# Re-ordered loads and weight sums in the first steps of a recurrent network kernel

## The chip, the cores and the metric

The kernel runs on one core of a Trainium2 chip. The core has five engines with a queue of instructions each: TensorE (PE, matrix products), VectorE (DVE), ScalarE (ACT), GpSimd (POOL) and SyncE (SP, which here only issues transfers). Transfers (DMAs) are issued on the queues of SP, ACT and POOL. The metric is the time of one execution on the device in microseconds (us); lower is better.

## The reference

A gated recurrent network runs over 128 time steps for 64 sequences; input and state have 512 values. The result is the input plus the state after each step.

```python
def step(h, inp):
    x_t, prop = inp
    comb = jnp.concatenate([x_t, h], axis=-1)
    z = jax.nn.sigmoid(comb @ Wz + bz)
    r = jax.nn.sigmoid(comb @ Wr + br)
    comb2 = jnp.concatenate([x_t, r * h], axis=-1)
    h_cand = jnp.tanh(comb2 @ Wh + bh)
    h_new = (1.0 - z) * h + z * h_cand
    h_next = jnp.where(prop, jnp.tanh(h_new @ Wp + bp), h_new)
    return (h_next, h_new)
```

`prop` holds for every fourth step. Each of Wz, Wr and Wh is 1024 x 512: its upper half multiplies x (in the kernel `wx`, 1.05 MB for each gate), its lower half multiplies the state (`wh[0]` for R, `wh[1]` for Z, `wh[2]` for H, 1.05 MB each). All values are float32.

## The kernel before

**Layout.** The 64 sequences are two halves of 32. A tile has 128 partitions: four quarters (`part(q)`) of a matrix's rows or of the 512 values, with 32 partitions each. All matmuls write 32 partitions, so that several run side by side.

**Two kinds of PE work.** The recurrent part of step t needs the state of step t-1: gates R, Z and H (`gate`), then PE multiplies for the half while the other half is in ACT and DVE. The input part (x times `wx`) does not depend on the state. It is cut into *units*, kept in a list (`put`), and taken from it between the recurrent gates (`fill`); how many are taken where stands in `PLACES`, in `HEAD` for steps 0 to 4 and in `TAIL`. `both(n)` takes n units for both halves at once, ahead of step 0. For steps 0 to 3 the units are plain products (`plain`, four per gate and step). From step 4 on the input part of several steps is computed together by a scheme of fewer products over sums of steps and sums of weights (`batch`); the first of these batches run in steps 1 and 2.

**Weight sums.** The batches need sums and differences of parts of `wx`. `sum_outer_1` makes `d5` (shown as `d` in the profile), `sum_outer` makes `tw[3]`, `tw[2]`, `tw[4]` in this order, two operations of 128x768 each; `sum_inner` and `sum_inner_1` make three sums (`tt`) and a fourth (`din`, or in place) of one weight, 128x384 each. Sums of x (`sum_raw12` gives `s12r`, `sum_raw34` gives `s34r`) stand on POOL too. Sums of weights 1 and 2 are made by DVE, all others by POOL. POOL's sums of weights 3, 5 and the outer ones start inside step 0: in `join` at t = 0 a copy of one element into `held` makes POOL wait until DVE has finished weight 2. `held` is used for such waits in two more places.

**The start, in order.** SP and ACT issue x of steps 0 and 1 (eight loads), the x part of Wr in two halves, Wz, Wh, then `wh[R]`; POOL issues the biases, h, and, after a `held` that waits for Wz, x of steps 2 and 3. A load takes one of eight semaphores in turn and waits until the load that had it before has landed. PE first runs 52 products of zeros (`idle`), then R of steps 0 and 1, the products that spread the three bias rows over the partitions (`spread`; ACT copies them to `bias_x`), then Z and H of these steps. `add_bias` (DVE) adds the biases and leaves the input part in `cp`; `seed` (ACT) copies it to the gate's place in PSUM, ahead of the recurrent products. `join_x` (DVE) transposes x of a step. Then four units of step 2 and step 0 itself. The products of one step share three scratch banks; `r_`, the gate R, lies in the bank of `scratch_r`, which the H units of an even plain step use as well.

The order on each engine is the order of the program text: there is no scheduler. The loop at the end interleaves the two halves by the number of columns that each has multiplied.

Of the kernel before, what the change touches and what calls it, by code (L numbers as in the profile page):

```python
# [18 lines left out]
def kernel(  # L19
# [14 lines left out]
    nc = tc.nc  # L34
# [97 lines left out]

    nc.gpsimd.tensor_copy(held, wx[0:1, 0, Z, 0:1])
    load_x(xr[0], 2, 2, 2, (nc.gpsimd, nc.gpsimd))

    dummy = const.tile([1, 1], F32, name="dummy")
    nc.scalar.activation(dummy, ones[:, 0:1], AF.Sigmoid)

    def load_wh(i):
        load_w(wh[i], gates_in[i][D:], engs=both_queues)  # L140

    load_wh(R)

# [130 lines left out]
    def inner(i, ka, na):  # L274
        return OPERAND[i](ka)[:, :, :, ts(na, J // 4)]
# [14 lines left out]

    def sum_outer():
        for ka in range(S):
            nc.gpsimd.tensor_sub(tw[3][:, ka], outer(1, 1, ka), outer(0, 1, ka))
            nc.gpsimd.tensor_add(tw[2][:, ka], tw[3][:, ka], outer(0, 0, ka))
            nc.gpsimd.tensor_sub(tw[4][:, ka], outer(1, 0, ka), tw[2][:, ka])

# [3 lines left out]

    def sum_inner(i, eng):
        eng.tensor_sub(tt[:, i - 1, 1], inner(i, 1, 1), inner(i, 0, 1))
        eng.tensor_add(tt[:, i - 1, 0], tt[:, i - 1, 1], inner(i, 0, 0))
        eng.tensor_sub(tt[:, i - 1, 2], inner(i, 1, 0), tt[:, i - 1, 0])

    def sum_inner_1(i, eng):
        eng.tensor_sub(leftover(i), inner(i, 0, 1), inner(i, 0, 0))

# [296 lines left out]
    )  # L605
    HEAD = {0: (4, 8, 0), 1: (8, 6, 0), 2: (16, 12, 0), 3: (8, 6, 8), 4: (6, 8, 0)}
    TAIL = {
# [9 lines left out]

    def plain_two(i):
        put(sum(map(list, zip(*(plain(t, (i,)) for t in range(2)))), []))
        both(2 * K)  # L620
# [70 lines left out]
    def behind_r(t, duo, u):  # L691
        odd = FIRST + 2 * duo + 1
        if t == 2:
            pair_left(0, 1, 2)
        elif t == 3:
            pair_right(0, 1, 10)
            sum_inner(7, nc.gpsimd)
            sum_inner_1(7, nc.gpsimd)
        if t == 4:
            sum_inner(4, nc.gpsimd)  # L700
            sum_inner_1(4, nc.gpsimd)
        if u == 0 and duo >= 1 and odd - 2 < LAST:
            outer_u2(odd - 2)

    def join(t, duo, u, n):
        even, odd = FIRST + 2 * duo, FIRST + 2 * duo + 1
        if t == 0 and n == 0:
            sum_inner(2, nc.vector)
            sum_inner_1(2, nc.vector)
            nc.gpsimd.tensor_copy(held, leftover(2)[0:1, 0, 0, 0:1])  # L710
# [15 lines left out]
    def behind_step(t, duo, u, h_new):  # L726
# [5 lines left out]
        if t == 0:  # L732
            sum_outer()
        if t == 3:
# [69 lines left out]
    def half(h):  # L804

        for t in range(T):
# [27 lines left out]
            if h == 1:  # L834
# [6 lines left out]
                if t == 1:  # L841
                    sum_raw34(1)
                    sum_inner(6, nc.gpsimd)
                    sum_inner_1(6, nc.gpsimd)
                if last:
                    nc.gpsimd.tensor_sub(xr[g][:, j], xr[g][:, j], keep)
                if t == 0:
                    join_x(1, 0)
                    join_x(1, 1)
                    sum_raw12(1)  # L850
                    sum_inner(5, nc.gpsimd)
                    sum_inner_1(5, nc.gpsimd)
                if t == 2:
# [97 lines left out]
```

## Time and profile before

| | us |
|---|---|
| runs shown | 1275.31, 1275.43, 1278.18 (median 1275.43) |
| the profiled execution | 1274.24 |
| its span on the core | 1272.4 |
| granted clock of PE, mean over the span | 0.997 of full |

The profile's page and trace come from the one profiled execution. Lines of the profile have the line of the kernel, the engine, the operation, the tiles written and read (`out<-in`), the shape and a count. In the stretches, each engine's busy time is followed by the number of its instructions in brackets; then come the clock granted to PE as a share of full speed, the share of the DMA engines that was busy, and GB/s. In the timeline a row has its start, its length, the engine and, in square brackets, how long the engine had been idle and what ended that. In the list of waits stand the instruction that waited, what it waited for, the time in total, how often, and the longest. Rows of DMA issues have the queue (SPq, ACTq, POOLq), the number of issues, the size of each and the median time from issue to landing. A float32 product stands twice in the trace. The line of most products, transposes and activations is that of a helper (L214 products, L240 activations of a gate, L384 `seed`, L422 `add_bias`, L256 `join_x`, L302 to L307 inner sums, L293 to L295 and L299 outer sums, L315 to L318 sums of x, L94 and L100 loads), so tiles tell them apart.

### The profile page before, as it was taken

The numbers are of one execution on the slowest core, as the hardware profiler recorded it, in microseconds if no ns is written. First come the engines' busy times: TensorE is split into PE (matmuls) and PEld (weight loads), VectorE is DVE, ScalarE is ACT, GpSimd is POOL, SyncE is SP. The second block draws the span as 40 slices with busy tenths as digits, with TensorE's granted clock in tenths as the row PEclk, the third lists the DMA queues.
The fourth block names the chain that finished last, engine by engine and source line by source line (L and its number), as shares of the span: only waits on it lengthen the run. The fifth ranks groups of instructions, "written<-read, shape, count | busy, mean of one in ns | idle before, by whom it ended". The sixth has DMA issues, their size and how long they took to land.

```text
span 1272.4 us, 60714 instructions
## 1 busy us (share of the span) xinstructions
PE 1253.4 (99%) x25964; PEld 1163.3 (91%) x25964; DVE 769.1 (60%) x2155; ACT 835.1 (66%) x2685; POOL 899.1 (71%) x1043
## 2 busy tenths in 40 slices
PE   8899999999999999999999999999999999999997
PEld 4688899999999999999999999999999999999875
DVE  2455666566666666656666666666666666666554
ACT  1456666766667666666666666666666666667665
POOL 2989767777677787767787677876777777677530
PEclk9999999999999999999999999999999999999999
DMA  9302212101221111112111121111111111111010
GB/s 234 92 3 53 52 42 62 38 22 51 52 53 36 38 49 38 53 36 57 40 28 52 50 55 36 36 40 49 53 37 47 41 37 53 41 48 36 11 43 19
DMA packets 112980, 60.82 MB, mean 48 GB/s; under 512 B 12968, under 2 KB 108968, under 8 KB 112712
## 3 DMA queue, kind: packets, MB, share of 16 engines
q1 hardware_dynamic: 109988, 53.20, 16.0%
q8 instruction: 205, 3.36, 1.1%
q10 hardware_dynamic: 2212, 3.34, 1.0%
q0 software_dynamic: 512, 0.40, 0.1%
q14 instruction: 63, 0.52, 0.1%
HBM read 40.11 MB, written 16.78 MB: 45 GB/s over the span
## 4 chain that ended last, share of the span: by engine, by line
PE 90%; POOL 5%; DMA 3%; issue 1%; DVE 1%; ACT 1%; SPq 0%; POOLq 0%; DVEq 0%; ACTq 0%
PE rec L214 41%; PE rec_z L214 15%; PE scratch_r L214 12%; PE scratch_q L214 10%; PE scratch_a L214 4%; PE scratch_y L214 4%; PE scratch_x L214 3%; DMA wh<-in_L_cond_Wz_dram 1%; DMA wx<-in_L_cond_Wh_dram 1%; POOL cp L555 1%; POOL mb L560 1%; DMA xr<-in_x_dram 0%; DMA wh<-in_L_cond_Wh_dram 0%; ACT rec_z L240 0%; DMA wx<-in_L_cond_Wr_dram 0%
## 5 line engine op out<-in xcount | busy, mean ns | idle before, releaser
L214 PE MATMUL rec<-wh,rhT 128*32 128x256 f32 x4096 | 375.5, 379 | 0.1
L214 PE MATMUL rec<-wh,hT 128*32 128x256 f32 x3072 | 281.6, 379 | 1.3 <-DVE hT L243 1.3
L214 PE MATMUL rec_z<-wh,hT 128*32 128x256 f32 x3072 | 281.6, 379 | 0.1
L214 PEld LDWEIGHTS rec<-wh,rhT 128*32 128x32 f32 x4096 | 249.8, 110 | 19.1 <-ACT scratch_r L240 0.5
L240 ACT ACTIVATE scratch_r<-rec 64x128 f32<-64x128 f32 x512 | 128.0, 250 | 131.7 <-PE rec L214 66.3
L384 ACT COPY rec<-cp 64x256 f32<-64x256 f32 x512 | 189.8, 371 | 25.1 <-DVE cp L422 5.7
L214 PEld LDWEIGHTS rec_z<-wh,hT 128*32 128x32 f32 x3072 | 192.4, 110 | 9.0 <-ACT rec_z L384 0.6
L214 PEld LDWEIGHTS rec<-wh,hT 128*32 128x32 f32 x3072 | 186.4, 110 | 14.1 <-ACT c L240 3.2
L240 ACT ACTIVATE rec_z<-rec_z 64x128 f32<-64x128 f32 x512 | 128.0, 250 | 98.8 <-PE rec_z L214 86.7
L240 ACT ACTIVATE c<-rec 64x128 f32<-64x128 f32 x512 | 138.9, 271 | 60.2 <-PE rec L214 48.8
L779 POOL TENSOR_TENSOR xr<-xr,h 128x256 f32<-128x256 f32 x127 | 92.8, 731 | 92.9 <-DVE h L872 81.9
L555 POOL TENSOR_TENSOR mb<-mb,mb 128x768 f32<-128x768 f32 x58 | 106.2, 1831 | 67.1 <-DVE mb L521 67.1
L555 POOL TENSOR_TENSOR cp<-mb,mb 128x768 f32<-128x768 f32 x76 | 138.9, 1827 | 8.1 <-DVE mb L521 4.4
L555 POOL TENSOR_TENSOR cp<-mb 128x768 f32<-128x768 f32 x46 | 84.2, 1830 | 56.8 <-ACT rec_z L384 55.4
L837 DVE SCALAR_TENSOR_TENSOR keep<-rec_z,h 128x256 f32<-128x256 f32 x96 | 40.7, 424 | 133.8 <-ACT rec_z L240 129.6
L214 PE MATMUL scratch_r<-tw,s 128*32 128x192 f32 x928 | 120.8, 326 | 0.0
L494 ACT COPY cq<-scratch_q 128x384 f32<-128x384 f32 x212 | 102.0, 481 | 19.9 <-PE scratch_q L214 18.4
L511 DVE TENSOR_TENSOR cx<-scratch_r,cx 128x384 f32<-128x384 f32 x106 | 59.0, 557 | 87.2 <-PE scratch_r L214 76.0
L214 PE MATMUL scratch_q<-tt,s 128*32 128x192 f32 x928 | 103.6, 326 | 0.0
L517 DVE TENSOR_TENSOR mb<-scratch_q,cx 128x384 f32<-128x384 f32 x106 | 59.0, 557 | 57.8 <-ACT cq L494 57.6
L821 DVE TENSOR_TENSOR rh<-scratch_r,h 128x128 f32<-128x128 f32 x192 | 56.0, 292 | 60.1 <-ACT scratch_r L240 60.1
L214 PE MATMUL rec<-wh,hpT 128*32 128x256 f32 x992 | 91.4, 379 | 0.1
(185 smaller groups left out, 3822.9 us busy)
## 6 DMA issues: line engine op xcount, KB each, us to landing
out_dram<-xr SPq DMA_DIRECT2D x249, 64.0 KB, 1.8
xr<-in_x_dram SPq DMA_DIRECT2D x248, 64.0 KB, 2.0
xs<-in_x_dram SPq DMA_DIRECT2D x240, 64.0 KB, 2.1
wp<-in_L_cond_Wp_dram SPq DMA_DIRECT2D x4, 256.0 KB, 5.0
wx<-in_L_cond_Wr_dram SPq DMA_DIRECT2D x4, 128.0 KB, 3.2
wx<-in_L_cond_Wr_dram ACTq DMA_DIRECT2D x4, 128.0 KB, 3.3
wx<-in_L_cond_Wz_dram SPq DMA_DIRECT2D x2, 256.0 KB, 5.9
wx<-in_L_cond_Wz_dram ACTq DMA_DIRECT2D x2, 256.0 KB, 6.6
```

The lines of the kernel that those rows point to most:

```text
L214: nc.tensor.matmul(ps[part(2 * h + c)], lhsT=left, rhs=rhs(c), start=start, stop=True, skip_group_check=True,)
L240: nc.scalar.activation(dst[ts(d, 2 * V)], gate_ps(i, h)[ts(h, 2 * V), d, :], func)
L384: nc.scalar.copy(gate_ps(i, h)[rows].rearrange("p d (c n) -> p d c n", c=C), G[t][rows, :, :, i, :].rearrange("p c d n -> p d c n"),)
L494: nc.scalar.copy(c[:, :nm], ps[:, :nm])
L511: nc.vector.tensor_add(T2[what][:, :nm], r_ps[:, :nm], T2[what][:, :nm])
L517: nc.vector.tensor_add(blocks(1, 1), runs(q_ps[:, :nm]), runs(T2[what][:, :nm]))
L555: nc.gpsimd.tensor_add(dst, a, b)
L560: nc.gpsimd.tensor_add(m, m, v.unsqueeze(1).to_broadcast([P, 2, 3 * J]))
L779: nc.gpsimd.tensor_add(xr[g][:, j], xr[g][:, j], h_new)
L821: nc.vector.tensor_mul(rh[:, h, :], r_, h_old[:, h, :])
L837: nc.vector.scalar_tensor_tensor(out=keep, in0=z, scalar=1.0, in1=h_old, op0=ALU.subtract, op1=ALU.mult)
```

## The change

1. x of steps 0 to 3 is loaded step by step (`load_step`, four loads of 32 KB each): step 0 first on SP and ACT, then the first half of Wr, then step 1 and the biases on POOL's queue, then the second half of Wr, Wz and Wh. Steps 2 and 3 follow on SP and ACT behind Wh and ahead of `wh[R]`. h waits for the second half of Wr instead of x. The activation table is loaded ahead of Wz's issue.
2. PE's start: 48 products of zeros for 52; R of step 0 and of step 1, first half of the depth; the biases; R, second half. Z and H of steps 0 and 1 step by step.
3. The inner sums are four operations in one function and can be done for some gates only: DVE makes weights 1 and 2 for R and Z as soon as these are loaded, and for H later, all before step 0. DVE also makes `d5` there (`sum_outer_1`), and POOL's `held` waits for it; POOL then does weights 3 and 5 and `tw[3]` ahead of step 0's own work, and `tw[2]`, `tw[4]` behind step 0.
4. Step 2's units: R and Z, then step 3, then H of step 2. Six units for four ahead of step 0, six for eight at its end. The H input part of step 0 is copied (`seed`) inside step 0.

```diff
+    def load_step(t, engs=both_queues):
+        for q in (0, 2, 1, 3):
+            engs[q // 2].dma_start(
+                out=xr[0][part(q), t], in_=x[:, t, ts(q, J)].rearrange("(h b) u -> b h u", h=S)
+            )
+    software_queue = (nc.gpsimd, nc.gpsimd)
...
-    load_x(xr[0], 0, 2, engs=both_queues)
-    for k in range(0, K, 2):
-        load_w(wx[:, :, R, :], gates_in[R][:D], k, k + 2, both_queues)
+    load_step(0)
+    load_w(wx[:, :, R, :], gates_in[R][:D], 0, 2, both_queues)
+    load_step(1, software_queue)
+    for i, b in enumerate((br, bh, bz)):
+        nc.gpsimd.dma_start(out=bias_row[:, i, :], in_=b.rearrange("(o n) -> o n", o=1))
+    load_w(wx[:, :, R, :], gates_in[R][:D], 2, K, both_queues)
+    dummy = const.tile([1, 1], F32, name="dummy")
+    nc.scalar.activation(dummy, ones[:, 0:1], AF.Sigmoid)
     for i in (Z, H_):
         load_w(wx[:, :, i, :], gates_in[i][:D], engs=both_queues)
-    for i, b in enumerate((br, bh, bz)):
-        nc.gpsimd.dma_start(out=bias_row[:, i, :], in_=b.rearrange("(o n) -> o n", o=1))
...
-    nc.gpsimd.tensor_copy(held, xr[0][0:1, 1, 1, 0:1])
+    nc.gpsimd.tensor_copy(held, wx[0:1, 2, R, 0:1])
...
-    nc.gpsimd.tensor_copy(held, wx[0:1, 0, Z, 0:1])
-    load_x(xr[0], 2, 2, 2, (nc.gpsimd, nc.gpsimd))
...
-    load_wh(R)
...
-    HEAD = {0: (4, 8, 0), 1: (8, 6, 0), 2: (16, 12, 0), 3: (8, 6, 8), 4: (6, 8, 0)}
+    HEAD = {0: (4, 6, 0), 1: (8, 6, 0), 2: (16, 12, 0), 3: (8, 6, 8), 4: (6, 8, 0)}
...
-    idle(52)
+    first = {i: [plain(t, (i,)) for t in range(2)] for i in (R, Z, H_)}
+    idle(48)
     join_x(0, 0)
+    now(first[R][0][:2])
     join_x(0, 1)
-    plain_two(R)
+    now(first[R][1][:2])
     spread(scratch[3], slice(0, 2), (R, H_))
     spread(scratch[1], slice(2, 3), (Z,))
+    nc.gpsimd.tensor_sub(bias_d, bias_x[:, 1], bias0)
+    load_step(2)
+    now(first[R][0][2:] + first[R][1][2:])
     for t in range(2):
         add_bias(t, (R,))
     for h in range(S):
         seed(R, 0, h)
-    load_wh(Z)
-    nc.gpsimd.tensor_sub(bias_d, bias_x[:, 1], bias0)
+    load_step(3)
+    load_wh(R)
+    now(sum(first[Z], []))
+    for i in (1, 2):
+        sum_inner(i, nc.vector, slice(0, 2))
+    for t in range(2):
+        add_bias(t, (Z,))
+    seed(Z, 0, 0)
     hT = new_T("hT", "hT_init")
     for h in range(S):
         turn(hT[:, h, :], h_init[:, h, :])
-    plain_two(Z)
-    for t in range(2):
-        add_bias(t, (Z,))
-    seed(Z, 0, 0)
+    load_wh(Z)
     join_x(0, 2)
-    sum_inner(1, nc.vector)
-    sum_inner_1(1, nc.vector)
-    plain_two(H_)
+    for i in (1, 2):
+        sum_inner(i, nc.vector, slice(2, 3))
+    now(sum(first[H_], []))
     for t in range(2):
         add_bias(t, (H_,))
-    for h in range(S):
-        seed(H_, 0, h)
     join_x(0, 3)
+    sum_outer_1(nc.vector)
+    nc.gpsimd.tensor_copy(held, d5[0:1, 1, 0, 0, 0:1])
+    for i in (3, 5):
+        sum_inner(i, nc.gpsimd)
+    sum_outer(3)
     load_wh(H_)
     later_loads()
-    put(plain(2) + plain(3))
-    both(K)
+    put(plain(2, (R, Z)) + plain(3) + plain(2, (H_,)))
+    both(6)
...
-        if t == 0 and n == 0:
-            sum_inner(2, nc.vector)
-            sum_inner_1(2, nc.vector)
-            nc.gpsimd.tensor_copy(held, leftover(2)[0:1, 0, 0, 0:1])
-            sum_inner(3, nc.gpsimd)
-            sum_inner_1(3, nc.gpsimd)
-            sum_outer_1(nc.gpsimd)
-        elif t == 1:
+        if t == 1:
             join_x(1, 2 + n)
...
         if t == 0:
-            sum_outer()
+            sum_outer(2)
+            sum_outer(4)
...
-            if last:
+            if last or t == 0:
                 seed(H_, t, h)
```

`now(units)` puts units on the list and takes them at once. `sum_outer(n)` makes `tw[n]` alone. The calls of `sum_inner_1` go with the new `sum_inner`, and `sum_inner(5, nc.gpsimd)` inside step 0 is gone.

More of the change, by code (lines that the diff above doesn't have):

```diff
@@ L131 @@
         )
-    nc.gpsimd.tensor_copy(held, wx[0:1, 0, Z, 0:1])
-    load_x(xr[0], 2, 2, 2, (nc.gpsimd, nc.gpsimd))
-    dummy = const.tile([1, 1], F32, name="dummy")
-    nc.scalar.activation(dummy, ones[:, 0:1], AF.Sigmoid)
     def load_wh(i):
         load_w(wh[i], gates_in[i][D:], engs=both_queues)
-    load_wh(R)
     xs = {}
@@ L289, in factor, with sum_outer @@
         }[j]()
-    def sum_outer():
+    def sum_outer(n):
         for ka in range(S):
-            nc.gpsimd.tensor_sub(tw[3][:, ka], outer(1, 1, ka), outer(0, 1, ka))
-            nc.gpsimd.tensor_add(tw[2][:, ka], tw[3][:, ka], outer(0, 0, ka))
-            nc.gpsimd.tensor_sub(tw[4][:, ka], outer(1, 0, ka), tw[2][:, ka])
+            if n == 3:
+                nc.gpsimd.tensor_sub(tw[3][:, ka], outer(1, 1, ka), outer(0, 1, ka))
+            elif n == 2:
+                nc.gpsimd.tensor_add(tw[2][:, ka], tw[3][:, ka], outer(0, 0, ka))
+            else:
+                nc.gpsimd.tensor_sub(tw[4][:, ka], outer(1, 0, ka), tw[2][:, ka])
     def sum_outer_1(eng):
@@ L299, in sum_outer_1, with sum_inner, of @@
             eng.tensor_sub(d5[:, ka], outer(0, 1, ka), outer(0, 0, ka))
[L301 to L307, printed above, removed]
+    def sum_inner(i, eng, gates=slice(0, 3)):
+        def of(v):
+            return v[:, :, gates]
+        t = [of(tt[:, i - 1, n]) for n in range(3)]
+        v = {ab: of(inner(i, *ab)) for ab in ((0, 0), (0, 1), (1, 0), (1, 1))}
+        eng.tensor_sub(t[1], v[1, 1], v[0, 1])
+        eng.tensor_add(t[0], t[1], v[0, 0])
+        eng.tensor_sub(t[2], v[1, 0], t[0])
+        eng.tensor_sub(of(leftover(i)), v[0, 1], v[0, 0])
     sx = {}
@@ L616, in both, with now @@
                     pass
-    def plain_two(i):
-        put(sum(map(list, zip(*(plain(t, (i,)) for t in range(2)))), []))
-        both(2 * K)
-    idle(52)
+    def now(units):
+        put(units)
+        both(len(units))
+    first = {i: [plain(t, (i,)) for t in range(2)] for i in (R, Z, H_)}
+    idle(48)
     join_x(0, 0)
+    now(first[R][0][:2])
     join_x(0, 1)
-    plain_two(R)
+    now(first[R][1][:2])
     spread(scratch[3], slice(0, 2), (R, H_))
     spread(scratch[1], slice(2, 3), (Z,))
+    nc.gpsimd.tensor_sub(bias_d, bias_x[:, 1], bias0)
+    load_step(2)
+    now(first[R][0][2:] + first[R][1][2:])
     for t in range(2):
@@ L843, in half @@
                     sum_inner(6, nc.gpsimd)
-                    sum_inner_1(6, nc.gpsimd)
                 if last:
@@ L850, in half @@
                     sum_raw12(1)
-                    sum_inner(5, nc.gpsimd)
-                    sum_inner_1(5, nc.gpsimd)
                 if t == 2:
```

2 lines of the change are left out of this document (removed).

## The prediction

> **What bounds the kernel now.** I read the page first, then the waits of TensorE (PE) over the whole span, then the first 120 us by stretches, because the change only touches the start.
>
> ```profile
> span 1272.4 us, 60714 instructions
> PE 1253.4 (99%) x25964; PEld 1163.3 (91%) x25964; DVE 769.1 (60%) x2155; ACT 835.1 (66%) x2685; POOL 899.1 (71%) x1043
> PE scratch_y L214 <- POOL s34r L317: 4.0, 1, 4.0
> PE scratch_q L214 <- DMA wx<-in_L_cond_Wr_dram: 2.2, 2, 1.3
> PE scratch_x L214 <- POOL s4r L317: 1.1, 1, 1.1
> PE rec L214 <- ACT rec L384: 1.0, 1, 1.0
> PE scratch_q L214 <- DVE cp L422: 0.7, 1, 0.7
> PE scratch_r L214 <- DVE rh L821: 0.3, 1, 0.3
> ```
>
> PE is busy 99% of the span: only what PE loses by waiting or by running slowly can be won. The longest wait, 4.0 us, is for one sum that POOL makes (`s34r`). In the stretches below the columns are PE, weight loads, DVE, ACT and POOL busy, then the clock granted to PE, the share of the DMA engines, and GB/s.
>
> ```profile
> 0.00:7.00 7.00, 4.89 (x56) 1.87 (x60) 1.04 (x3) 0.00 (x0) 3.46 (x11) 1.00 0.60 169
> 7.00:14.15 7.15, 5.20 (x80) 2.56 (x80) 0.62 (x2) 2.49 (x6) 2.65 (x6) 1.00 1.03 264
> 14.15:19.00 4.85, 4.85 (x60) 3.24 (x64) 0.54 (x3) 0.66 (x2) 2.82 (x5) 0.65 1.06 253
> 19.00:26.10 7.10, 5.89 (x108) 3.46 (x99) 4.15 (x10) 0.75 (x3) 0.00 (x0) 1.00 1.06 292
> 35.00:56.00 21.00, 20.76 (x421) 15.54 (x412) 12.28 (x36) 12.01 (x40) 20.40 (x18) 1.00 0.37 95
> 56.00:61.00 5.00, 1.21 (x16) 0.80 (x20) 1.39 (x4) 0.00 (x0) 4.92 (x7) 0.85 0.26 72
> 61.00:66.00 5.00, 5.00 (x98) 3.65 (x94) 0.13 (x1) 0.96 (x2) 4.84 (x6) 0.81 0.13 33
> 66.00:110.00 44.00, 44.00 (x956) 39.16 (x952) 26.18 (x72) 27.26 (x87) 40.33 (x44) 1.00 0.14 35
> ```
>
> Three limits follow each other. Up to 26 us the loads decide: the DMA engines are full at 253 to 292 GB/s. From 35 to 61 us POOL is never idle while PE catches up with it and waits. From 66 us PE is full.
>
> **The wait at 60 us.** POOL's chain and PE around it:
>
> ```profile
> 32.56 0.17 POOL L710 COPY held<-din 1x1 f32<-1x1 f32 x1 [15.50 <-DVE din L307]
> 32.88 1.01 POOL L302 TENSOR_TENSOR tt<-wx 128x384 f32<-128x384 f32 x1
> 36.97 3.63 POOL L299 TENSOR_TENSOR d<-wx 128x768 f32<-128x768 f32 x2
> 40.54 0.48 POOL L315 TENSOR_TENSOR s12r<-xT 128x128 f32<-128x128 f32 x1
> 42.35 1.00 POOL L302 TENSOR_TENSOR tt<-d 128x384 f32<-128x384 f32 x1
> 46.44 1.85 POOL L293 TENSOR_TENSOR tw<-wx 128x768 f32<-128x768 f32 x1
> 57.66 0.72 POOL L779 TENSOR_TENSOR xr<-xr,h 128x256 f32<-128x256 f32 x1
> 59.28 0.45 POOL L317 TENSOR_TENSOR s34r<-xT 128x128 f32<-128x128 f32 x1
> 44.53 0.33 PE L214 MATMUL scratch_x<-tt,s12r 128*32 128x192 f32 x2
> 59.79 0.54 PE L214 MATMUL scratch_y<-tt,s34r 128*32 128x192 f32 x2 [4.03 <-POOL s34r L317]
> 62.97 0.33 PE L214 MATMUL scratch_q<-wx,xT 128*32 128x192 f32 x2
> ```
>
> POOL sits idle 15.5 us until DVE has made `din`, and then works without a break from 32.88 to 59.73, when `s34r` is ready. Its pieces, by the differences of the starts: inner sums of weight 3 take 4.09, the outer difference `d` 3.57, `s12r` 1.81, inner sums of 5 another 4.09, six outer sums 11.22 (two of each kind, so 3.7 a pair). PE stood from 55.76 to 59.79 and then ran until 62.97 with matmuls of 0.54 instead of 0.33 us; the clock there was half (0.81 on average over five microseconds). Three microseconds at half rate lose 1.6.
>
> **Price of the wait: 4.0 + 1.6 = 5.6 us.** After the change POOL's gate (`held`) waits for `d5`, which DVE makes before step 0 instead of inside it, and `d` is no longer POOL's. When does DVE finish it?
>
> ```profile
> 23.65 0.56 DVE L303 TENSOR_TENSOR tt<-tt,wx 128x384 f32<-128x384 f32 x1
> 25.19 0.42 DVE L422 TENSOR_TENSOR cp<-scratch_r,bias_x 128x256 f32<-128x256 f32 x1
> 25.85 0.43 DVE L256 STREAM_TRANSPOSE xT<-xr 128x256 f32<-128x256 f32 x1
> 7.34 0.64 PE L214 MATMUL scratch_a<-wx,xT 128*32 128x256 f32 x8
> 7.77 0.64 PE L214 MATMUL scratch_q<-wx,xT 128*32 128x256 f32 x8
> 12.00 1.06 PE L186 MATMUL scratch_x<-tt,ones 1*32 1x512 f32 x8
> 26.12 1.96 PE L214 MATMUL rec<-wh,hT_init 128*32 128x256 f32 x28 [1.02 <-ACT rec L384]
> ```
>
> The sums by gates make 16 DVE operations of eight: eight of 256 elements (not shown for two operands from SBUF; between the 0.42 of a 256-element bias add and the 0.56 of 384 elements: 0.45 taken) and eight of 128 (at most 0.42; 0.32 taken). `d5` is two of 768 elements: between 0.56 each (the 384-element row) and 1.8 each (POOL's row); I take 1.0, near twice the 384-element row, which is the nearest. In DVE's new order, from the landing of Wz at 13: 3.6 for R and Z, bias adds 0.8, turns and the transpose of step 2 about 1.5, sums of H 2.6, giving 21.5; the two bias adds of H 0.8, transpose 0.4, `d5` 2.0, giving about 24.7, and the transpose waits for the x of step 3, so I allow 25.5. POOL then starts 7.4 us earlier than 32.88. `s12r` now stands behind weights 3 and 5 and one outer pair: 25.5 + 8.2 + 3.7 + 1.8 = 39.2. `s34r` is ready at 59.73 - 7.4 - 3.6 = 48.7. PE wants the first at 44.53 and the second at 55.76, less what it gains before; with the 3.5 below that is 41.0 and 52.3. So slacks of 1.8 and 3.6 us: **the 5.6 us go.** What is late next is `s4r` near 112 us, 1.1 us. That stays: POOL's chain before it hangs on results of PE in step 2 and later, and moves with PE.
>
> **The head.** A unit (8 rows of matmul) takes 7.77 - 7.34 = 0.43 us, so a gate of two steps 3.44. A weight matrix of 1.05 MB at 264 GB/s takes 4.0. x of two steps, h, Wr and Wz are 2.5 MB; 169 GB/s moved 1.2 of it in the first 7 us, the rest takes 5.0, and with about 1 us for the last landing Wz is there at 13 and Wh at 17 (estimates from these rows). The rows for what comes behind:
>
> ```profile
> 11.95 2.29 SPq L100 DMA_DIRECT2D wh<-in_L_cond_Wr_dram  x2
> wh<-in_L_cond_Wr_dram SPq DMA_DIRECT2D x2, 256.0 KB, 8.7
> wh<-in_L_cond_Wh_dram ACTq DMA_DIRECT2D x2, 256.0 KB, 5.1
> xr<-in_x_dram POOLq DMA_DIRECT2D x8, 32.0 KB, 7.0
> tt<-in_L_cond_br_dram POOLq DMA_DIRECT2D x1, 2.0 KB, 2.1
> DVE xT L256 <- DMA xr<-in_x_dram: 2.7, 1, 2.7
> ```
>
> - *x of step 0 alone ahead of Wr; four fillers less.* Wr is issued sooner, and of the 2.2 us that PE waits for Wr most can go. Nothing of that is kept: Z must wait for Wz, which is a matter of bytes. h, now behind Wr, is wanted only by the turns at about 17.
> - *x of step 1 and the biases on POOL's queue.* Landing 2.1 (the small row) to 7.0 us (the full engines' row) after an issue at about 3: 5 to 10 us. Behind it PE has 0.9 + 1.5 (the bias matmuls, 12.00 to 13.5) + 1.7; Wz lands at about 13, so up to 8.5 is free and 10 costs 1.5, which the wait for wh of R below takes up. Taken: 0.
> - *Biases spread between the halves of R*: the bias adds no longer hold up Z (the 0.7 us for `cp`); hidden by Wz too. Bias matmuls that came late would cost what x of step 1 costs.
> - *x of steps 2 and 3 behind the input weights, on SP and ACT.* DVE waited 2.7 us for them. Now eight more DMAs stand ahead of wh. The built order shows that the four on ACT's queue, and wh of R behind them, wait for the landings of Wh (each new DMA reuses the semaphore of an older one). Wh lands at about 17, so ACT's half of wh of R goes out at about 18.3 and, at the 5.1 us of a lightly loaded landing, is there at 23.4 to 24. Before, SP's last was issued at 13.9 (11.95 + 2.29, less 0.3 for the issue) and landed 8.7 later, at 22.6. Bounds: 22 (bytes only, an earlier start) to 27 (18.3 + 8.7). Taken: 24.
> - PE: Z 13 to 16.4, H (Wh at 17) to 20.5, six units of step 2 to 23.1, wait, gate R of step 0 at 24.2. **Before: 26.12, so 1.9 gained**; two more units are done by then (the 6 for 4), **0.9**; and the 0.3 for `rh` (ACT's sigmoid stood behind the issue of wh of H) goes, start to start about **0.6**. Sum 3.4. The 1.02 us at 26.12 (sums ahead of the bias adds of H, whose copies gate R waited for) is inside the 1.9.
> - *Six for eight units in step 0's end*: the same units, earlier. Each half still has 1.3 us of units and 0.9 of the other half's gate over about 1.9 us of sigmoid, DVE and turn; without that cover 0.3.
>
> The clock is a second matter. Row 14.15:19.00 shows 0.65 although PE hardly waited there: the bias matmuls use one row. The change has such a stretch too, with a wait of some 2 us; one half-rate stretch of 3.4 us would cost 1.7, and the wait for wh of R takes up about 1.1: 0.6 off the sum. The Trainium skill ("TensorE: Matmul & The Clock Gate", "What's actually happening") puts the drop at an idle window of about 3.4 us. The half rate behind the 4.03 us wait agrees; the 0.65 row does not, and the measurement decides. By the rule alone the new head would stay at full clock and the sum below would stand whole.
>
> **Sum.** 5.6 + 3.4 = 9.0 us. The profiled execution took 1274.24 us with a span of 1272.4; less 9.0 it is 1265.2. The median of the runs shown, 1275.43, is 1.2 above the profiled one, so I forecast **1266.0** for the median (the sum gives 1266.4; the units start to start give PE's wait at 60 us a few tenths more).
>
> **Rivals.**
> - *The loads keep to the bytes.* If the new waits never empty the queues, wh of R lands at 22.3 and R starts when PE is ready, at 23.1: 1.1 more. For it: 253 to 292 GB/s whatever queue issues. **1264.9**. The Trainium skill ("DMA: Bandwidth & Descriptors", "Issuing engines are not separate DMA queues") says that all queues run on the same 16 engines and only issue time is saved; by it no load gets faster by moving, and none slower; the rows of this case agree as to the bandwidth.
> - *wh of R late.* At 27 by the bound above: 2.8 of the 3.4 go. **1269.0**.
> - *POOL late.* `d5` behind a late x of step 3: every microsecond beyond 1.8 is PE's wait for `s12r`, with half a clock window behind it; 3 us give 1.2, and 1.6 if the clock falls too. **1269.0**.
> - *It does nothing:* both of these together and the clock. **1272 to 1275**.
> - *Slower: ACT's queue starves the loads.* Half of wh of Z and H is issued by ACT behind a copy that waits for DVE's bias add of Z, behind eight sums, behind Wz. PE needs wh of H at about 32 us; each microsecond of landing beyond that is lost. It decides from a landing at 32 + 9 = 41 on (by 0.3% from 45). Against it: ACT's copy is due at about 18, and one issued then would be there by 27 even at 8.7. **1280**.
>
> **Chances.** Forecast 0.62 (its own range 1264 to 1268.5), bytes only 0.13, wh of R late 0.09, POOL late 0.07, nothing 0.05, slower 0.04. The range reaches from 1262.5 (bytes only, and the runs as near to the profiled one as it was) to 1270. A difference of 0.3%, 3.8 us, is about what a measurement tells from none. Faster by more 0.90, within 0.06, slower 0.04.
>
> **What would show it.** PE's wait for `s34r` gone and no half clock behind it; `held` released at 24 to 26 by `d`; gate R of step 0 at 23 to 25, released by wh of R; POOL idle for some microseconds before the sums of step 4; the 1.1 us for `s4r` still there. I am wrong if PE waits for `s12r`, if R starts after 26, or if the clock falls a second time before 30 us.

## The result and the profile after

The changed kernel takes **1270.72 us** (median of five runs, 1268.43 to 1271.65) beside 1276.22 for the kernel before on the same chip (five runs, 1275.31 to 1278.18): a ratio of **0.9951, 95% interval 0.9937 to 0.9966**. That is 4 to 8 us gained where 9.4 were forecast. The time stands 0.7 above the upper end of the range; taken by the ratio on the 1275.43 from which the prediction started, it is 1269.2.

The profiled execution took 1271.65, only 2.6 below the 1274.24 of the profile before. That is below each of the five runs of the kernel before beside it, while this one is the longest of its own five, so the two traces show less than the medians do. The page of the changed kernel:

```profile
span 1269.8 us, 60717 instructions
```

Where did the time go? DVE makes `keep` once a step, behind gate Z, so its start marks how far a step has come. Steps 0, 2 and 3 in the timeline of DVE, first before, then after:

```profile
35.76 0.42 DVE L837 SCALAR_TENSOR_TENSOR keep<-rec_z,h_init 128x256 f32<-128x256 f32 x1 [2.34 <-ACT rec_z L240]
...
55.97 0.42 DVE L837 SCALAR_TENSOR_TENSOR keep<-rec_z,h 128x256 f32<-128x256 f32 x1 [0.59 <-ACT rec_z L240]
76.03 0.42 DVE L837 SCALAR_TENSOR_TENSOR keep<-rec_z,h 128x256 f32<-128x256 f32 x1 [1.68 <-ACT rec_z L240]
```

```profile
39.42 0.42 DVE L850 SCALAR_TENSOR_TENSOR keep<-rec_z,h_init 128x256 f32<-128x256 f32 x1 [4.56 <-ACT rec_z L244]
...
58.76 0.42 DVE L850 SCALAR_TENSOR_TENSOR keep<-rec_z,h 128x256 f32<-128x256 f32 x1 [0.59 <-ACT rec_z L244]
73.04 0.43 DVE L850 SCALAR_TENSOR_TENSOR keep<-rec_z,h 128x256 f32<-128x256 f32 x1 [1.67 <-ACT rec_z L244]
```

The changed kernel is 3.66 us *late* in step 0, 2.79 in step 2, and 2.99 *early* in step 3. From there on little changes: the rest of the span is 1196.4 us before and 1196.8 after. So 5.8 us were won between steps 2 and 3 (the wait for `s34r`), 0.9 behind step 0 (two units fewer at its end, put ahead of it), and 3.66 lost before. The head, which was to give 3.4, took 2.8 net in this pair of traces. PE's waits after:

```profile
PE rec L218 <- DMA wh<-in_L_cond_Wr_dram: 3.2, 1, 3.2
PE scratch_r L218 <- DMA xr<-in_x_dram: 1.9, 1, 1.9
PE scratch_x L218 <- POOL s4r L327: 1.1, 1, 1.1
```

`s34r` is gone, `s4r` stands as it was, and the longest wait is a new one, for wh of R. The stretches:

```profile
14.15:19.00 4.85, 3.02 (x56) 1.89 (x48) 3.67 (x11) 0.00 (x0) 0.00 (x0) 1.00 0.94 200
19.00:26.10 7.10, 6.25 (x112) 4.28 (x112) 4.99 (x14) 1.12 (x3) 0.00 (x0) 1.00 0.83 227
26.10:28.58 2.48, 0.00 (x1) 0.03 (x2) 0.23 (x1) 0.00 (x0) 1.84 (x3) 1.00 1.06 232
28.58:36.00 7.42, 7.42 (x104) 5.21 (x108) 1.85 (x6) 2.48 (x8) 7.18 (x8) 0.77 0.89 179
56.00:61.00 5.00, 5.00 (x126) 4.96 (x121) 3.08 (x9) 2.76 (x10) 4.45 (x4) 1.00 0.02 5
```

At 56 to 61 us PE is full where it had 1.21 of 5 us. But from 14 to 26 us the loads move 200 and 227 GB/s instead of 253 and 292, PE does nothing from 26.1 to 28.58, and behind that the clock falls. PE's timeline in the head:

```profile
13.51 1.93 PE L218 MATMUL scratch_q<-wx,xT 128*32 128x256 f32 x32 [0.55 <-DVE cp L432]
19.12 1.93 PE L218 MATMUL scratch_r<-wx,xT 128*32 128x256 f32 x32 [1.95 <-DMA xr<-in_x_dram]
22.57 2.80 PE L218 MATMUL scratch_q<-wx,xT 128*32 128x256 f32 x48
28.58 2.74 PE L218 MATMUL rec<-wh,hT_init 128*32 128x256 f32 x28 [3.21 <-DMA wh<-in_L_cond_Wr_dram]
31.10 0.64 PE L218 MATMUL rec<-wh,hT_init 128*32 128x256 f32 x2
33.13 0.39 PE L218 MATMUL scratch_q<-wx,xT 128*32 128x256 f32 x2
```

Z starts at 13.5, H at 19.1, the six units at 22.6, gate R of step 0 at **28.58** (before 26.12, forecast 24.2), and from 29.6 to 33.0 a product takes 0.64 instead of 0.39. (Rows in between are left out here and in the other timelines. H's wait is shown as one for x; Wh, which H needs, landed last at 18.87 in the trace.) The issues on SP and ACT tell why; the second column is the time from the first of a group to the end of the last:

```profile
11.55 2.52 SPq L114 DMA_DIRECT2D xr<-in_x_dram  x4
17.55 2.38 SPq L100 DMA_DIRECT2D wh<-in_L_cond_Wr_dram  x2
15.02 4.19 ACTq L114 DMA_DIRECT2D xr<-in_x_dram  x2
...
20.31 2.32 ACTq L100 DMA_DIRECT2D wh<-in_L_cond_Wr_dram  x2
20.44 1.72 SPq L100 DMA_DIRECT2D wh<-in_L_cond_Wz_dram  x2
```

Between 14.1 and 17.5 us nothing new but one load of 32 KB goes out. wh of R, issued from 11.0 to 13.9 before, goes out from 17.55 to 22.2, its last two beside wh of Z, and the last of it lands at 28.4. That SP itself waited for a landing of Wh stands in its list of waits:

```profile
SPq L100 <- DMA wx<-in_L_cond_Wh_dram: 3.5, 1, 3.5
```

Last, DVE and POOL:

```profile
20.82 0.45 DVE L260 STREAM_TRANSPOSE xT<-xr 128x256 f32<-128x256 f32 x1 [2.76 <-DMA xr<-in_x_dram]
24.54 1.78 DVE L306 TENSOR_TENSOR d<-wx 128x768 f32<-128x768 f32 x2
26.47 0.17 POOL L667 COPY held<-d 1x1 f32<-1x1 f32 x1 [13.73 <-DVE d L306]
67.97 0.46 POOL L325 TENSOR_TENSOR s12r<-xT 128x128 f32<-128x128 f32 x1 [7.43 <-PE scratch_r L218]
```

DVE waits 2.76 us for x of step 2, until 20.8. `held` is released by `d` at 26.5, two operations of 0.89 us that start at 24.5, and POOL later stands 7.4 us idle.

### The profile page after: what moved, and what is told of

The parts are those of the page before. It is cut to its first block, busy times and chain, and to the rows that moved or that the text cites. A ratio compares the mean times of both kernels' runs of the same rounds, so it can differ in the third digit from the quotient of the medians.

```text
span 1269.8 us, 60717 instructions
## 1 busy us (share of the span) xinstructions
PE 1251.8 (99%) x25960; PEld 1164.5 (92%) x25960; DVE 772.3 (61%) x2165; ACT 835.7 (66%) x2685; POOL 893.1 (70%) x1036
## 3 DMA queue, kind: packets, MB, share of 16 engines
q10 hardware_dynamic: 2372, 3.41, 1.2%
## 4 chain that ended last, share of the span: by engine, by line
PE 92%; POOL 2%; DMA 2%; issue 1%; ACT 1%; DVE 1%; SPq 0%; ACTq 0%; POOLq 0%; DVEq 0%
PE rec L218 42%; PE rec_z L218 15%; PE scratch_r L218 13%; PE scratch_q L218 10%; PE scratch_a L218 5%; PE scratch_y L218 4%; PE scratch_x L218 4%; DMA wx<-in_L_cond_Wh_dram 1%; POOL cp L565 1%; POOL mb L570 1%; DMA wh<-in_L_cond_Wr_dram 0%; DMA xr<-in_x_dram 0%; DMA wx<-in_L_cond_Wr_dram 0%; ACT rec_z L244 0%; SPq L802 0%
## 5 line engine op out<-in xcount | busy, mean ns | idle before, releaser
L504 ACT COPY cq<-scratch_q 128x384 f32<-128x384 f32 x212 | 102.1, 482 | 19.7 <-PE scratch_q L218 18.3
```

The costliest lines, as they stand in the source:

```text
L504: nc.scalar.copy(c[:, :nm], ps[:, :nm])
```

## The experiments

All were timed in five runs, in turn with nine of the kernel before on the same chip (five of it beside the changed kernel). The runs of one kernel lie 1 to 4 us apart, so a difference of two kernels below about 1.5 us is not told apart.

| run | median, us | kernel before | ratio, 95% interval |
|---|---|---|---|
| the changed kernel | 1270.72 | 1276.22 | 0.9951 (0.9937 to 0.9966) |
| sums_only | 1270.38 | 1276.41 | 0.9948 (0.9935 to 0.9960) |
| x23_pool | 1267.14 | 1276.41 | 0.9930 (0.9917 to 0.9942) |
| wh_first | 1268.36 | 1276.41 | 0.9936 (0.9924 to 0.9948) |
| cover24 | 1270.86 | 1276.41 | 0.9952 (0.9938 to 0.9965) |
| cover60 | 1270.83 | 1276.36 | 0.9955 (0.9941 to 0.9968) |
| wh_first_late6 | 1267.44 | 1276.36 | 0.9929 (0.9917 to 0.9942) |
| x23_on_sp | 1270.80 | 1276.36 | 0.9961 (0.9949 to 0.9974) |
| bias_behind_r | 1268.09 | 1276.36 | 0.9933 (0.9921 to 0.9946) |
| sums_cover | 1270.66 | 1277.20 | 0.9949 (0.9935 to 0.9962) |
| after_cover2 | 1269.58 | 1277.20 | 0.9941 (0.9928 to 0.9953) |
| late6_cover | 1267.39 | 1277.20 | 0.9928 (0.9914 to 0.9941) |
| sums_reorder | 1268.93 | 1275.36 | 0.9950 (0.9936 to 0.9964) |

The theory: the sums give what was forecast, and the head loses because the loads of x of steps 2 and 3 stand ahead of wh of R. The rivals: the loads are a matter of bytes wherever they stand; the loss is the clock's; the sums cost the head something.

**sums_only.** The kernel before with the change's part 3 alone.

```diff
     plain_two(Z)
+    for i in (1, 2):
+        sum_inner(i, nc.vector, slice(0, 2))
...
     join_x(0, 3)
+    sum_outer_1(nc.vector)
+    nc.gpsimd.tensor_copy(held, d5[0:1, 1, 0, 0, 0:1])
+    for i in (3, 5):
+        sum_inner(i, nc.gpsimd)
+    sum_outer(3)
```

The sums that these replace are taken out, as in the change.

> The kernel before with the weight sums alone changed (sums of weights 1 and 2 by gates on DVE, d5 on DVE, POOL's gate behind d5, outer pairs split); loads and the order of step 0's units as before. Theory (the sums give their 5.6 us and only the head of the changed kernel lost): the 4.0 us wait for s34r and the half clock behind it are gone, gate R of step 0 starts within 0.5 us of the 26.1 of before, and the time is 5.6 us below the kernel before, near 1270.6. Rival (the sums cost DVE or POOL something in the head): gate R of step 0 starts a microsecond or more later and the gain is 3 to 4.5 us.

Measured: 6.0 us below the kernel before, as much as the whole change; no wait for `s34r`. So the rest of the change is worth nothing on balance. Gate R started at 27.85, later than expected. PE came to it without a wait, for it had run at half rate; but x of steps 2 and 3, which DVE needs ahead of the last bias adds, had landed late as well (24.1, before 22.3), and these adds ended only at 27.66. Wz, which no sum stands ahead of, landed 0.8 to 1.7 us later than in the trace before, so the sums are not shown to have cost the head anything. The stretches, the clock in the third column from the end:

```profile
7.90:11.31 3.41, 1.43 (x28) 0.74 (x24) 0.00 (x0) 0.52 (x1) 0.00 (x0) 1.00 0.99 268
11.31:14.73 3.42, 3.42 (x32) 1.45 (x28) 0.00 (x0) 0.97 (x2) 1.82 (x4) 0.50 1.07 276
14.73:18.14 3.41, 3.31 (x29) 0.98 (x24) 2.08 (x5) 1.76 (x5) 3.31 (x7) 0.50 1.06 239
18.14:21.55 3.41, 3.41 (x36) 1.58 (x32) 3.15 (x8) 0.00 (x0) 0.34 (x1) 0.50 1.06 255
```

Three half-rate stretches instead of the one at 15 us before: the same start of loads and products can lose 1.7 or 5 us of PE to the clock, from run to run. (Step 2's `keep` stands 1.7 us later here than before.)

**x23_pool.** The changed kernel with x of steps 2 and 3 back on POOL's queue.

```diff
+    nc.gpsimd.tensor_copy(held, wx[0:1, 0, Z, 0:1])
+    for t in (2, 3):
+        load_step(t, software_queue)
...
-    load_step(2)
...
-    load_step(3)
```

> The changed kernel with x of steps 2 and 3 back on POOL's queue behind the landing of Wz, as the kernel before has it; all else as changed. Theory (the eight loads of x ahead of wh of R, and their waits for landings on ACT, made wh of R land at 28.4): wh of R lands at 22 to 24, gate R of step 0 starts at 23 to 25 instead of 28.6, no half clock behind it, and the time is 5 to 6 us below the changed kernel, 1264 to 1266. Rival (bytes and split loads of x, Wr and biases fill the DMA engines whatever the order): wh of R still lands at 27 or later and the time is within 1.5 us of the changed kernel's 1270.7.

Measured: 1267.14, 3.6 us below the changed kernel by the medians, 2.7 by the ratios (0.9930 to 0.9951; the two intervals just overlap). Issues on SP and PE's timeline:

```profile
11.07 2.50 SPq L100 DMA_DIRECT2D wh<-in_L_cond_Wr_dram  x2
```

```profile
19.69 1.93 PE L222 MATMUL scratch_r<-wx,xT 128*32 128x256 f32 x32 [2.48 <-DMA wx<-in_L_cond_Wh_dram]
23.14 2.80 PE L222 MATMUL scratch_q<-wx,xT 128*32 128x256 f32 x48
25.73 1.96 PE L222 MATMUL rec<-wh,hT_init 128*32 128x256 f32 x28
```

wh of R goes out from 11.1 to 13.3 and the last of it lands at 24.7, later than expected but a microsecond before it is wanted; gate R follows the six units without a wait, 2.85 us earlier, and the clock stays full. The bytes rival falls. The time is above the expected 1264 to 1266, for H waits 2.48 us for Wh, which landed at 19.4. PE loses 4.6 us to waits in this head (0.64, 0.97, 0.51, 2.48); in the changed kernel it loses 0.35, 1.00, 0.55, 1.95 and 3.21 and half of a 3.4 us stretch, 8.8 together. The difference, 4.2, is close to the 4.5 that `keep` of step 3 is earlier by (68.51 for 73.04).

**wh_first.** The changed kernel, `load_wh(R)` ahead of `load_step(2)`.

```diff
+    load_wh(R)
     load_step(2)
...
     load_step(3)
-    load_wh(R)
```

> The changed kernel with wh of R issued ahead of x of steps 2 and 3 on SP and ACT; all else as changed. Theory (order on the two queues): wh of R lands at 22 to 23 and gate R of step 0 starts at 23 to 25 whenever x of step 2 is there too, for the six units of step 2 stand ahead of it; time 1264 to 1267. If x of steps 2 and 3 now land late (25 or more), d5 and POOL start later and PE waits for the units or for s12r instead: 1268 to 1271. Rival (bytes): no change, 1270 to 1272.

Measured: 1268.36, by the ratios 1.9 us below the changed kernel, in the band expected for a late x: the six units wait 1.53 us for x of step 2. The profiled run was the fastest of the five (1266.82). Issues of SP, then PE:

```profile
10.10 2.30 SPq L100 DMA_DIRECT2D wh<-in_L_cond_Wr_dram  x2
14.76 3.36 SPq L114 DMA_DIRECT2D xr<-in_x_dram  x4
```

```profile
17.65 1.93 PE L218 MATMUL scratch_r<-wx,xT 128*32 128x256 f32 x32 [1.68 <-DMA wx<-in_L_cond_Wh_dram]
22.84 2.80 PE L218 MATMUL scratch_q<-wx,xT 128*32 128x256 f32 x48 [1.53 <-DVE xT L260]
25.45 1.93 PE L218 MATMUL rec<-wh,hT_init 128*32 128x256 f32 x28
```

wh of R now lands at 20.3 and Wh at 17.5, earlier than in x23_pool too. The stretch ahead of H moves more here than there; x23_pool first, then wh_first (the last column is GB/s):

```profile
15.58:18.99 3.41, 1.62 (x32) 0.85 (x24) 2.29 (x7) 0.38 (x1) 1.94 (x3) 1.00 1.06 252
```

```profile
14.47:17.88 3.41, 1.73 (x33) 0.98 (x29) 2.63 (x9) 0.00 (x0) 0.00 (x0) 1.00 1.04 342
```

The same loads on the same queues as in the changed kernel, in another order, bring wh of R 8 us earlier. Gate R gains 3.1; it stands behind the six units, and these wait for x of step 2.

**x23_on_sp.** Is it ACT's waiting, or the eight loads wherever they are?

```diff
-    load_step(2)
+    load_step(2, (nc.sync, nc.sync))
...
-    load_step(3)
+    load_step(3, (nc.sync, nc.sync))
```

> The changed kernel with x of steps 2 and 3 on SP's queue alone (eight loads there, none on ACT), still ahead of SP's half of wh of R. If ACT's waits for landings ahead of its half of wh of R are what made it late, ACT's half is issued near 14 and lands by 21, SP's half lands at 23 to 25, gate R starts at 24.5 to 26 and the time is 1266 to 1268.5. If it is enough that eight loads stand ahead of wh of R anywhere, wh of R still lands at 27 to 28.5 through SP's half and the time is 1269.5 to 1271.

Measured: 1270.80, nothing regained. The issues on SP, then on ACT, and PE:

```profile
10.61 8.14 SPq L114 DMA_DIRECT2D xr<-in_x_dram  x8
18.79 0.91 SPq L100 DMA_DIRECT2D wh<-in_L_cond_Wr_dram  x2
```

```profile
18.19 0.93 ACTq L100 DMA_DIRECT2D wh<-in_L_cond_Wr_dram  x2
```

```profile
27.65 2.56 PE L218 MATMUL rec<-wh,hT_init 128*32 128x256 f32 x28 [2.98 <-DMA wh<-in_L_cond_Wr_dram]
```

ACT had nothing ahead of wh of R here after 13 us, and yet issued it at 18.19. A load takes one of eight semaphores and waits for the load that had it before. Seven of the eight small loads of x take those of Wz and Wh, the eighth one of x of step 2, and the four of wh of R have to wait for one landing of Wh (18.17 in the trace, for ACT's first) and three of x of step 2 (18.56 to 18.90), which came in behind Wh. So it is not ACT's queue alone, as the prediction had it, but the number of loads between Wz and wh of R. In wh_first wh of R takes Wz's semaphores, which come free from 9.1 to 12.1 us; in x23_pool POOL's loads use others.

**wh_first_late6.** wh_first with the six units behind gate R.

```diff
-    both(6)
...
-                yield from fill(2 * K, h)
+                yield from fill(2 * K + 6, h)
```

> wh of R ahead of x of steps 2 and 3 as in the run before, and the six units of step 2 moved behind gate R of step 0 (22 units there instead of 16). Theory: in that run wh of R was there at 20.3 and TensorE then stood 1.5 us for the transposed x of step 2; without the six units ahead gate R starts at 21 to 22, where H ends, and the 1.5 us go: 1266 to 1267 against 1268.4 for the run with wh of R first. Rival (what is late next): rh of step 0 stands on DVE behind d5 and the 22 units end before it, or the units wait for x of step 2, and the wait only moves: 1268 to 1269.

Measured: 1267.44, between the two expectations and not told apart from wh_first. The wait for x of step 2 is gone, but in the profiled run the clock fell:

```profile
16.44:19.86 3.42, 1.44 (x31) 0.92 (x28) 1.37 (x5) 0.00 (x0) 0.00 (x0) 1.00 1.04 305
19.86:23.27 3.41, 3.41 (x40) 2.17 (x35) 0.00 (x0) 1.12 (x3) 0.00 (x0) 0.50 0.66 165
```

**cover24, cover60 and after_cover2**: the changed kernel with products of zeros into a free bank where PE waits, 24 or 60 ahead of gate R; in the last, 28 ahead of H and 56 ahead of gate R. They add products whose results nothing uses.

```diff
+    def cover(n):
+        for i in range(n):
+            nc.tensor.matmul(
+                scratch[4][part(i % NQ)], lhsT=zeros[:, :V], rhs=zeros, start=True, stop=True
+            )
...
+    cover(28)
     now(sum(first[H_], []))
...
     both(6)
+    cover(56)
```

> The changed kernel with 24 idle products (about 2.6 us by the 0.43 us of four in its start) on TensorE between the six units of step 2 and gate R of step 0, into a bank that nothing uses then; no load moves. If the half clock at 29.6 to 33.0 comes from the 3.2 us wait, the idle products remove it, gate R still starts at 28.6 and the time falls by 1.7 us, to about 1269.0. If the half clock has another cause, it stays and the time is within 0.5 us of 1270.7.

> As the run with 24 idle products, but with 60 of them (four took 0.21 to 0.25 us there, so about 3.2 us), so that TensorE is busy nearly up to gate R of step 0. If the half clock behind that wait comes from the wait, it is gone, gate R runs at 0.39 us a product at 28.4 to 29.0, and the time falls by 1 to 1.7 us against the changed kernel's 1270.7 (less a few tenths where the products end after wh of R has landed): 1269.0 to 1269.8. If the half clock has another cause, it stays behind 28 us and the time is within 0.5 us of 1270.7.

> The changed kernel with 28 idle products before gate H's units (the wait for Wh, about 1.5 of its 2 to 2.5 us) and 56 before gate R of step 0 (about 3.0 us), so that no stretch of 3.4 us has more than some 1.2 us without products of full width. Theory (the clock's part of the loss): no half clock before 36 us in the profile, gate R at 27.5 to 29, time 1269.0 to 1269.8 against 1270.7, and the rest of the loss, some 3 us, stays, for wh of R is as late as before. Rival (idle products delay as much as they save, or the half clock has another cause): within 0.5 us of 1270.7.

cover24 tells nothing: the 24 products took 1.5 us, not 2.6, PE still waited 2.2, and the half clock stayed. In cover60 none followed gate R, but one came earlier, at 18.8 to 22.2, behind a wait of 2.5 us ahead of H; the time was 1270.83. The 60 products also ran until 29.7 and held gate R back to 29.49, though the last of wh of R had landed at 27.3 in that trace, so this run does not price the clock. Only with both waits covered was the clock full in the whole head:

```profile
18.66 1.93 PE L224 MATMUL scratch_r<-wx,xT 128*32 128x256 f32 x32 [0.60 <-DMA wx<-in_L_cond_Wh_dram]
27.73 1.96 PE L224 MATMUL rec<-wh,hT_init 128*32 128x256 f32 x28
```

after_cover2 took 1269.58, as expected of the theory, with runs from 1269.09 to 1270.23, closer together than all others. Its gain of 1.1 us is small against the intervals; it has the sign and about the size that one stretch of 1.7 us in most runs would give. The rest of the loss stays, for the loads stand in the order of the changed kernel. In this trace wh of R landed at 26.2, and gate R started behind the 56 products at 27.73, so the cover itself cost about 1.5 us there.

**late6_cover.** wh_first_late6 with 28 products of zeros ahead of H.

```diff
+    cover(28)
     now(sum(first[H_], []))
```

> wh of R ahead of x of steps 2 and 3, the six units of step 2 behind gate R (as in the run before), and 28 idle products before gate H's units. Theory: the half clock at 19.9 to 23.3 behind the 1.98 us wait for Wh goes, gate R of step 0 at 21 to 22.5 instead of 23.8, time 1265.3 to 1266.5 against 1267.4. Rival (loads bound it, and the run's spread is theirs): 1267 to 1268.

Measured: 1267.39, no gain. The clock was full and gate R started at 22.67 (23.81 in the run before), but Z had waited 1.21 us for Wz, and PE 0.3 us for `s12r`: POOL starts its sums only at 29.5, as x of step 3 and `d5` behind it are late now. `keep` of step 0 is 1.0 us earlier than in the run before, that of step 1 only 0.3. This fits the rival, that the loads bound this order.

**sums_cover, sums_reorder and bias_behind_r** ask what the rest of the head gives once x of steps 2 and 3 is out of the way (x23_pool against sums_only: 3.2 us by the medians, 2.3 by the ratios). sums_cover is sums_only with 36 products of zeros in the wait for Wr and 12 behind each block of bias products; sums_reorder is sums_only with the change's part 4; bias_behind_r is x23_pool with the `spread` calls behind all of R.

```diff
-    plain_two(R)
+    put(sum(map(list, zip(*(plain(t, (R,)) for t in range(2)))), []))
+    both(K)
+    cover(36)
+    both(K)
     spread(scratch[3], slice(0, 2), (R, H_))
+    cover(12)
     spread(scratch[1], slice(2, 3), (Z,))
+    cover(12)
```

```diff
-    for h in range(S):
-        seed(H_, 0, h)
...
-            if last:
+            if last or t == 0:
                 seed(H_, t, h)
...
-    put(plain(2) + plain(3))
-    both(K)
+    put(plain(2, (R, Z)) + plain(3) + plain(2, (H_,)))
+    both(6)
```

```diff
-    spread(scratch[3], slice(0, 2), (R, H_))
-    spread(scratch[1], slice(2, 3), (Z,))
-    nc.gpsimd.tensor_sub(bias_d, bias_x[:, 1], bias0)
     now(first[R][0][2:] + first[R][1][2:])
+    spread(scratch[3], slice(0, 2), (R, H_))
+    spread(scratch[1], slice(2, 3), (Z,))
+    nc.gpsimd.tensor_sub(bias_d, bias_x[:, 1], bias0)
```

> The kernel before with the weight sums alone changed, and idle products into a free bank on TensorE where it waits in the head: 36 (about 1.9 us) before the second half of gate R's units, 12 behind each of the two blocks of one-row bias products. No load moves. Theory (what is left of the head's gain, once x of steps 2 and 3 stays where it was, is the clock: in the run with the sums alone three half-rate stretches followed the 1.98 us wait for Wr and the one-row products): no half clock before gate R of step 0, gate R at 25 to 26.5 instead of 27.85, and the time 1268 to 1269.2 against 1270.4. Rival (the gain comes from the earlier Wr and from x by step): the half clock goes but the time stays within 0.7 us of 1270.4, for the loads bound the head.

> The run with the sums alone, and with it the changed order of step 0: copies of the biases of H behind gate R of step 0 instead of ahead of it, the six units of step 2 (R and Z first) ahead of gate R and six behind gate H instead of eight and eight. All loads as in the kernel before. Theory A (this order carries what the head of the changed kernel gains beside its loads: gate R no longer waits about 1 us for the copies of H's biases, and rh no longer waits about 1 us on its way): gate R is not released by ACT, the time is 1268.4 to 1269.6 against 1270.4. Theory B (the rest of the head's gain, some 3 us between the run with the sums alone and the run with x of steps 2 and 3 on POOL's queue, is in x by step, Wr ahead and the biases between): the time is within 0.7 us of 1270.4.

> The run with x of steps 2 and 3 back on POOL's queue, and the one-row bias products moved behind all of gate R's units of steps 0 and 1, where the kernel before has them. If the head's gain came from the one-row products no longer standing in one block with the waits (the kernel before and the run with the sums alone show half clock in that stretch), a half clock of 3.4 us or more comes back between 11 and 22 us and the time rises by 1.5 to 3 us against 1267.1. If their place does not matter (the bias adds of R hidden behind the landing of Wz, as the prediction has it), the time is within 0.7 us of 1267.1.

sums_cover: the half clock was gone in the whole head, the time was not lower (1270.66, ratio 0.9949 for 0.9948). With that order of the loads gate R waits anyway:

```profile
24.56 1.93 PE L220 MATMUL scratch_q<-wx,xT 128*32 128x256 f32 x32 [0.71 <-DVE xT L262]
27.44 1.96 PE L220 MATMUL rec<-wh,hT_init 128*32 128x256 f32 x28 [0.95 <-ACT rec L396]
32.20 0.41 PE L220 MATMUL scratch_r<-wx,xT 128*32 128x256 f32 x2 [1.12 <-DVE rh L837]
```

sums_reorder: the last two of these waits are gone from the trace, but the ratio is 0.9950, the same as sums_only; its median is 1.4 us lower beside a kernel before that was 1.0 lower. bias_behind_r: 1.0 us above x23_pool, with no half clock in its head; H waited 3.4 us for Wh there, which landed at 20.2. Neither the bias products' place nor the order of step 0 shows a gain of its own that five runs can tell; what each of the head's other edits gives stays open.

## Why the prediction came out as it did

- **The wait at 60 us: right.** 5.6 us forecast, 5.8 in the traces, 6.0 by sums_only alone. POOL started at 26.8 instead of 25.5, because x of step 2 was late (DVE took it up at 20.8) and all that follows on DVE with it; x of step 3 cost only 0.2 more. The slack of `s34r` bore that, as PE was later too. POOL then stands 7.4 us idle before the sums of step 4, and `s4r` keeps its 1.1 us, as said. The sizes held: DVE's `d5` took 0.89 us an operation for the 1.0 that was taken.
- **The head: wrong, and by one step,** the arrival of wh of R ("Taken: 24"). It was to win 3.4 us and lost 2.8, and gate R behind 26 us was one of the prediction's own signs of being wrong; that the time still came out at the edge of the range is owed to the sums' part and to the range's width. Each part of that sum was too short: Wh landed at 18.9, not 17; the last of wh of R went out at 22.2, not 18.3; and it took 6.3 us, not 5.1, with wh of Z beside it. Of the 3.9 us at the issue 1.9 are Wh's landing; the issue of the load just ahead on ACT took another 1.8 us, from 20.31 to 22.14, and what held it is not shown. The bound of 27 (18.3 + 8.7) came nearer, but by a landing time that was too long. The prediction saw that new loads wait for the semaphores of older ones, but counted that wait for ACT's queue alone: x23_on_sp and SP's own wait of 3.5 us in the changed kernel show that the eight loads use up the eight semaphores, so that SP's half waits as well. Between 14.1 and 17.5 us hardly anything is issued, and from 17 to 21 us the transfers move 97 to 180 GB/s in each microsecond, where they moved 236 to 291 before.
- **The rival "wh of R late"** (0.09) named what happened, at 27 and 1269.0. It came at 28.4, and the half clock came on top.
- **The clock.** "The wait for wh of R takes up about 1.1" assumed a half-rate stretch ahead of that wait. It came behind it, where nothing covers it: the full 1.7 us. (The 0.6 that the prediction priced for the clock is not in its sum of 9.0 either.) Gate R at 28.58 for 24.2, and 1.7: 6.1 us, against the 6.2 between the 3.4 gained in the forecast and the 2.8 lost in the trace.
- **"Bytes only"** (0.13) had the order of the loads without effect, on the condition that the waits never empty the queues. That did not hold, as just said. wh_first moves the same bytes on the same queues and has wh of R 8 us earlier. Over all traces the last of wh of R landed at 26.2 to 28.4 in the order of the changed kernel (x on SP alone included), at 24.7 and 26.0 with x on POOL's queue, and at 20.3 to 21.9 with wh of R first. The Trainium skill ("DMA: Bandwidth & Descriptors", "Issuing engines are not separate DMA queues") states that all queues share the same 16 engines; x23_on_sp agrees in that moving x between SP and ACT changes nothing. Loads that are held back before they are issued are another matter, and they decide here.
- **The terms at nothing.** x of step 0 ahead of Wr, and the biases between: PE now waits 1.00 us for x of step 1 (8.60), and Z still waits for `cp`, but Z starts at 13.51, just behind the landing of Wz at 13.26, so next to nothing is lost, as said. Without the move of x the other edits of the head give 2.3 to 3.2 us over sums_only. That is near the 3.4 forecast, but partly by luck, for sums_only lost 1.7 us to the clock in its own head. Beside the trace before, x23_pool's head is 1.7 ahead (`keep` of step 2 at 54.23 for 55.97): 0.4 at gate R where 1.9 were forecast, since H waited for Wh, 0.5 up to `keep` (0.6 forecast), and the 0.9 of the two units. Which edit gives what was not settled.
- **The start value.** The forecast took the profiled execution as 1.2 below the median. Over the study the medians of the kernel before were 1275.4 to 1277.2, so it was 1 to 3 below. sums_only shows a possible reason: the same head with three half-rate stretches instead of one.

The best versions are x23_pool (1267.14) and wh_first_late6 (1267.44, and 1267.39 with the covered wait): some 3 us below the changed kernel and 9 below the kernel before.

## What to carry to other kernels

Count the loads, not only the bytes, between two large ones: with a fixed number of semaphores taken in turn, many small loads in a row make the next large one wait for landings, on whichever queue it stands. Put the load whose landing ends the longest wait ahead of small ones that have slack, and read the time of its *issue* first. A wait of 2 to 3 us on PE can cost another 1.7 us, if the clock falls behind it; here that depended on how the wait lay in the clock's grid.

## What the runs showed of the hardware

*The clock.* It falls on a grid of 3.41 us whose start differs from run to run, and less idle time is enough than a whole stretch of it. Two stretches of the same length, one of the changed kernel with full clock behind it, and (shown above, 16.44) one of wh_first_late6 with half clock behind it:

```profile
15.96:19.37 3.41, 1.46 (x30) 0.78 (x26) 1.93 (x6) 0.12 (x1) 0.00 (x0) 1.00 0.86 203
26.20:29.61 3.41, 1.03 (x16) 0.81 (x20) 0.12 (x1) 0.00 (x0) 2.79 (x4) 1.00 1.07 235
29.61:33.02 3.41, 3.41 (x39) 2.22 (x34) 0.60 (x2) 1.24 (x5) 3.28 (x4) 0.50 1.07 217
```

At full clock, PE busy for 1.46 us or more of the stretch kept the clock (also 1.62 in x23_pool and 1.73 in wh_first, shown above, 1.67 and 1.75 in bias_behind_r); 1.44 or less lost it (1.43 in sums_only, 1.21 in x23_on_sp, 1.20 in cover24, 1.03 in the changed kernel, 0.90 in cover60). In bias_behind_r a wait of 3.41 us lay across two stretches and cost no clock at all. The bias products with one row do not seem to count as busy: before, the stretch ahead of the half clock at 15.16 was busy for 2.75 us, 1.5 of them with these, and sums_reorder shows the same (2.75 us busy, half rate behind it at 15.81). Two stretches of sums_only, shown above, fit only if time at half rate counts half as well: from 11.31 and from 14.73 PE was busy for 3.42 and 3.31 us, and half rate followed all the same; without the bias products (13.66 to 16.45 us) 2.4 and 1.6 us are left, at half rate. That is a reading of a few stretches and was not tried by itself. The Trainium skill ("TensorE: Matmul & The Clock Gate", "What's actually happening") puts the half rate behind an idle window of about 3.4 us that runs freely; the grid and its changing start agree, the amount of idle time does not: some 2 us of the 3.41 were enough.

*The transfers.* Small loads of x in between seem to cost more than their bytes: 252 GB/s in x23_pool and 342 in wh_first, in the stretches shown above, with the same kind of large loads under way. That was seen, not tried by itself.
